# Two-layer attention kernel: attention weights times values by row halves, and a new order at the seams

## The chip, the core and the metric

The kernel runs on one core of a Trainium2 chip. A core has a matrix engine (TensorE, PE in the profile, with its weight loads as PEld), a vector engine (VectorE, DVE), a scalar engine (ScalarE, ACT), GpSimd (POOL) and SyncE (SP), which only starts transfers. Each engine works through its own list of instructions in order; engines wait for one another by semaphores. Transfers are started from the queues of SP, ACT and POOL and run on 16 DMA engines. Matmuls read SBUF and write PSUM, which has eight banks of 2 KB per partition; ACT and DVE read the results there.

The metric is the time of one execution on the device in microseconds (us). The clock granted to TensorE is given in the profile as a share of full speed.

## The reference

Two layers, each added to its input after a group normalisation, on two images of 256 channels and 64 x 64 positions, in float32. The first is full attention with 8 heads of 32 channels over all 4096 positions. The second has three parts, cut to what matters:

```
q, k, v = 1x1 convolutions of the normalised input (conv1, conv2, conv3)
fq, fk  = q, k plus a position term

# "lr": attention among the 64 blocks of 8 x 8 positions, for each place in a block
att   = softmax(fq^T fk / 16);  ctx = att v            # 64 groups of 64 tokens
feats = relu(bn(lr_W ctx))

# "sr": attention among the 64 positions of each block
qx = relu(bn(fq2 relu(bn(fq1 feats)))),  kx likewise,  vx = fv feats
ctx2   = softmax(qx^T kx / 16) vx                      # 64 groups of 64 tokens
feats2 = relu(bn(sr_W ctx2))

out = x + rate1 * feats2 + rate2 * depthwise_conv3x3(fc-mix of q, k, v)
```

## The kernel before

`direct_layers` does all of it; `general_layers` (the last third of the file) is compiled but only runs when a row sum of the first softmax falls out of range, which it doesn't here. For each image b the kernel goes through four stages: normalise and project (`group_stats`, `normalise`, `project0`), full attention (`attention0`), `layer1_first` with the lr attention, `layer1_second` with the sr attention and the convolution. The positions are cut into NT = 8 tiles of T = 512, the channels into KC = 2 chunks of P = 128.

Inside `manual_schedule` blocks the order of the PE instructions is the order of the code; elsewhere, and for the other engines, a scheduler places instructions by its own estimate of when their inputs are there. `issue_after(x)` holds what stands in it back until the instruction x. Where two blocks meet, the scheduler may set the first matmuls of the next among the last of the one before.

**group_attention** (line 982 on) handles eight groups of 64 tokens at once. It is a generator whose caller advances it, so that other work can be put between its steps. `sp` (L1012, with a small extra product of 5 rows, L1018) computes the scores, two groups at a time in the two column halves of the array. DVE and ACT make the softmax (L1028 to L1035). PE turns the weights (`at`, L1040), so that the tokens summed over lie on the partitions: two groups on partitions 0 to 63 and 64 to 127. DVE copies them in two instructions of 64 partitions (L1049) into `bd`, a block diagonal matrix for each pair w of groups: group 0's weights in the upper left, group 1's in the lower right, zeros elsewhere (set once by POOL). `pc` (L1058) is then, for each output chunk m and each pair w, one 128 x 128 by 128 product with `vs`, the values of both groups, in a bank for each m. Then `out(m, pc)` runs: ACT scales, shifts and clips (`bn_relu`, L1069) from PSUM into `feats` (lr) or `res` (sr). A float32 matmul is two pairs of instructions in the trace, so the 8 products of a group are 16 records. There are 8 calls per stage and image: 32 in all.

In the lr loop the call of tile t is interleaved with the projection `py` of tile t+2 (`project`, L1108) and with the `pc` of tile t-1. In the sr loop a tile first runs the q branch (`phq`, `prq`), perhaps a step of the convolution, the k branch (`phk`, `prk`), the attention, and more steps of the convolution at the places in `spots`. A convolution step is `mm` (L931), 16 products whose inputs `v` POOL prepares from the padded image `xp`, and whose results `z` DVE adds to the tiles of x (L936 to L958). Its weights `wf` are made by DVE, kept in DRAM and fetched at the first step of image 0 (sr tile 2); `pw` (L890) then mixes them on PE. `give(n)` (L1251) adds a finished tile of sr and starts the 512 KB output transfer.

**Seams.** `load_x` starts eight 512 KB loads on SP's queue. At the start POOL's queue carries the constants, 16 small loads of projection biases (L115) and then the first weights wqk. `fold_scores` (L186) multiplies weights w1, w2 and the position rows into one matrix for the lr scores; it stands after `project0` of image 0 and before its attention, and its first short part (`pt_place`, `pt_meet`, `pt_key`) is a chain between PE and ACT. `finish_last` ends the first attention: DVE takes the reciprocal of 128 x 512 row sums (L625) from ACT's copy `kept`, multiplies, adds x, and takes the last of the statistics; then `pm_l` and `pv_l` on PE turn statistics into mean and variance, and `firsts` are the first halves (chunk 0) of the first `py` products, put there for the time that normalising chunk 1 takes. `following` (L1349) starts the loads of image 1 in the last sr tile of image 0 and takes their statistics (`bn_stats`, L308, 16 instructions on DVE; aggregate L312).

Of the kernel before, what the change touches and what calls it, by code (L numbers as in the profile page):

```python
# [9 lines left out]
F32 = mybir.dt.float32  # L10
# [30 lines left out]
def direct_layers(ctx: ExitStack, tc: tile.TileContext, a: dict, out: bass.AP, bad: bass.AP):  # L41
# [34 lines left out]

    x_first = load_x(0)


    by_out = {}  # L80
    for name in ("w1", "w2"):
        by_out[name] = wpool.tile([P, KC, C], F32, tag="wp", name=f"{name}_by_out")

        for i in range(4):
# [4 lines left out]
            )  # L89
    place_rows = w4([4, C], "place_rows")  # L90
    nc.sync.dma_start(out=place_rows, in_=a["posq"])
    grid = const.tile([2, 64], F32, name="grid")
    nc.sync.dma_start(out=grid, in_=a["loc"][1:3, 0:64])
    meet = const.tile([2, P], F32, name="meet")
# [16 lines left out]
    for nm, col in (("wk0", V_BK0), ("wq0", V_BQ0)):  # L111
        b0[nm] = const.tile([P, 2], F32, name="b_" + nm)
        for h in range(NH0):
            r = HD0 * (h % 4)
            nc.gpsimd.dma_start(  # L115
                out=b0[nm][r : r + HD0, h // 4 : h // 4 + 1],
                in_=a["vecs"][64 * (h % 2) : 64 * (h % 2) + HD0, col + h // 2 : col + h // 2 + 1],
            )
# [67 lines left out]
    def fold_scores():  # L186


        wts["g"] = wpool.tile([P, KC, C], F32, tag="wp", name="wt_g_0")

# [24 lines left out]
        nc.tensor.matmul(pk, meet, grid, start=True, stop=True)  # L215
        nc.scalar.copy(at_key, pk)
        for k in range(KC):
            block = slice(k * P, (k + 1) * P)
            pg = bank([P, C + AT], f"pt_g_{k}")
            product(pg[:, 0:C], lambda j: by_out["w1"][:, j, block], lambda j: by_out["w2"][:, j, :])  # L220
            product(pg[:, C : C + 2], lambda j: by_out["w1"][:, j, block], lambda j: place[:, j, 1:3])
            product(pg[:, C + 2 : C + AT], lambda j: by_out["w2"][:, j, block], lambda j: part[:, j, :])
            nc.scalar.copy(wts["g"][:, k, :], pg[:, 0:C])
            nc.scalar.copy(w_at[:, k, 0:AT], pg[:, C : C + AT])
        nc.sync.dma_start(out=kept_w["g"], in_=wts["g"])

    outer = {}
# [59 lines left out]

    bd = const.tile([P, 4, 2, 64], F32, name="bd0")
    nc.gpsimd.memset(bd, 0.0)
    bds = [bd, bd]  # L290
    turn = [0]


    class Stats:
# [35 lines left out]

    def group_stats(xts, tagn):
        st = Stats(xts, tagn)
        for t in range(NT):
            for k in range(KC):
                st.tile(k, t)
        both, pv = slice(0, KC), bank([P, KC], f"pv_{tagn}")
        st.aggregate(both)
        st.means(both, bank([P, KC], f"pm_{tagn}"), nc.vector.tensor_copy)
        st.spread(both)
        st.variances(both, pv)  # L340
        st.deviations(both, pv)
        return st.mean, st.rstd

# [113 lines left out]
    def attention0(b, xts, held):  # L457
# [117 lines left out]
        def sum_rows(g, rows):  # L575
            if g == last:
                for j in SUMMED_LAST:
                    quarters(rows, ones, lambda u: unit(g, j, u), j == SUMMED_LAST[0], False)
                quarters(rows, ones, lambda u: acc[u], False, False)
            quarters(rows, ones, lambda u: added[g][u // 2][:, u % 2, :], g < last, True)  # L580

# [29 lines left out]
        def finish_last(g):  # L611
# [9 lines left out]
            st.shift = shift  # L621
            shift_of(st, 0)
            kept = w4([P, T], f"kept_{b}")
            nc.scalar.copy(kept, rows)
            nc.vector.reciprocal(avs[:, 1, :], kept)  # L625
            y = avs[:, 0, :]
            nc.scalar.copy(y, sums[g])
            nc.vector.tensor_mul(y, y, avs[:, 1, :])
            nc.vector.scalar_tensor_tensor(y, y, bv_last, held["x_last"], ALU.add, ALU.add)
# [351 lines left out]

    def group_attention(nm, q, k, tokens, wv, out, busy=False, apart=False, more=None):

# [60 lines left out]

        bd = bds[turn[0] % 2]
        turn[0] += 1
        for tt in range(2):
            rows = slice(64 * tt, 64 * tt + 64)
            nc.vector.tensor_copy(  # L1049
                bd[rows, :, tt, :].rearrange("p (a u) i -> p u a i", a=2), at[rows]  # L1050
            )
        if apart:
            values(1)
        yield
        for m in range(KC):
            pc = bank([P, T], f"pc_{nm}_{m}")
            for w in range(4):
                nc.tensor.matmul(  # L1058
                    pc[:, w * P : (w + 1) * P], vs[:, w, m * P : (m + 1) * P],
                    bd[:, w].rearrange("p a i -> p (a i)"), start=True, stop=True,  # L1060
                )
            out(m, pc)

# [4 lines left out]
    def bn_relu(dst, src, col, m):  # L1068
        nc.scalar.activation(  # L1069
            dst, src, AF.Relu, bias=vecs[:, col + 2 + m : col + 3 + m], scale=vecs[:, col + m : col + m + 1]  # L1070
        )


    def layer1_first(b, xts, put, check, st):
# [64 lines left out]
        with tc.manual_schedule(engines={E.PE, E.Activation, E.DVE}):  # L1139
# [14 lines left out]
            st.spread(second)  # L1154
            firsts = [lambda t=t, m=m: project(t, m, slice(0, 1)) for t in range(2) for m in range(KC)]
            if b:
# [20 lines left out]
        with tc.manual_schedule(engines={E.PE}):  # L1177

            before = None
            for t in range(NT + 1):  # L1180
                parts = None
                if t < NT:
                    def to_feats(m, pc, t=t):
                        bn_relu(
                            feats[m][:, :, t, :].rearrange("p o e -> p e o"),
                            pc.rearrange("p (e o) -> p e o", e=8), V_LR, m,
                        )

                    rows = slice(HD0 * (t % 4), HD0 * (t % 4) + AT)
                    parts = group_attention(  # L1190
                        f"lr_{b}_{t}", tiles.pop(t), source(t),
                        lambda c, w, t=t: source(t)[:, c, w * P : (w + 1) * P], wts["w3"], to_feats, b == 0,
                        more=(queries[rows, t // 4, :], keys[t // 4][rows, :], t == 0, t >= NT - 2),
                    )
                    next(parts)
                    if t == 3:
                        at_grid(1)
                for m in range(KC):
                    if t + 2 < NT:
                        project(t + 2, m, slice(0, KC))  # L1200
                    if before:
                        next(before, None)
                    if m == 0 and NT - 2 <= t < NT:
                        next(parts)
# [6 lines left out]
    def layer1_second(b, xts, feats, mean, rstd, shift, pacc, following):  # L1211
# [40 lines left out]
        def give(n):  # L1252
            res = results.pop(n)
            for m in range(KC):
                nc.vector.scalar_tensor_tensor(
                    res[:, m, :], res[:, m, :], wts["rate1"], xts[n][:, m, :], ALU.mult, ALU.add
                )
            nc.sync.dma_start(out=out[b, :, n * T : (n + 1) * T].rearrange("(k p) n -> p k n", p=P), in_=res)

        if b:  # L1260
            for t in range(3):
                to_image(t, True)
            ahead[0] = conv_transform(b, xp, *turns[0])
        pending = None
        for t in range(NT):
# [25 lines left out]
            with tc.manual_schedule(engines={mybir.EngineType.PE}):  # L1291
# [5 lines left out]
                for tt in images.get(t, ()):  # L1297
                    to_image(tt)
                if 0 in spots.get(t, ()):
                    conv()  # L1300
                if b == 0 and t == NT - 1:
                    for n in sorted(results):
                        give(n)
                k = branch("fk1", "fk2", V_FK1, V_FK2, "k")
                res = w4([P, KC, T], f"res_{nt}")

                def to_res(m, pc, res=res):

                    bn_relu(
                        res[:, m, :].rearrange("p (d o e) -> p o d e", d=8, o=8),  # L1310
                        pc.rearrange("p (o d e) -> p o d e", o=8, d=8), V_SRW, m,
                    )

                parts = group_attention(
                    nt, q, k, lambda c, w, f=f: f[c][:, w * P : (w + 1) * P], wts["fv"], to_res, apart=t + 1 < NT
                )
# [5 lines left out]
                else:  # L1322
                    next(parts)
                    if b == 0 and t == NT - 1:
                        following()
                    next(parts, None)
                if 2 in spots.get(t, ()):
                    conv()
# [20 lines left out]
    def following():  # L1349
        xts = load_x(1)  # L1350
        ahead.update(xts=xts, w0=load_layer0(1), stats=group_stats(xts, "l0_1"))

    for b in range(B):
        xts = x_first if b == 0 else ahead["xts"]
        w0 = w0_first if b == 0 else ahead["w0"]
        with tc.tile_pool(name=f"ps0_{b}", bufs=8, space=PSUM) as psum["ps"]:
            mean, rstd = group_stats(xts, "l0_0") if b == 0 else ahead["stats"]
            xn = apool.tile([P, KC, N], F32, tag="A", name=f"xn_{b}")
            for t in range(NT):
                for k in range(KC):  # L1360
                    normalise(xn[:, k, t * T : (t + 1) * T], xts[t][:, k, :], k, mean, rstd)
            held = project0(b, xn, w0)
            if b == 0:
                fold_scores()
        if b == 0:
# [569 lines left out]
```

## Time and profile before

| what | value |
|---|---|
| median of 3 runs | 3122.33 us (3120.56 to 3123.84) |
| profiled execution: its own time | 3121.84 us |
| its span, first to last instruction | 3120.1 us |
| mean granted clock of TensorE | 0.992 |
| attention of image 0, 110 to 1150 us: PE busy | 1035.70 of 1040.00 us |
| lr of image 0, 1150 to 1280: PE busy | 121.77 of 130.00 us |
| sr of image 0 with what follows, 1280 to 1660: PE busy | 365.40 of 380.00 us |
| attention of image 1, 1690 to 2705: PE busy | 1009.47 of 1015.00 us |

The profile is one execution, recorded by the chip. The span is cut into stages by time, and for each stage the table of windows gives the busy microseconds of each engine. A group line gives instructions of one line and shape with their number, and a second column with the shortest, median and longest duration in ns or the busy sum and mean. A wait line gives who waited for whom, and the total, number and longest of these waits. In a line in order of time the first number is the start, the second the length until the last record's end; the bracket is the idle time ahead of it, with what ended it.

### The profile page before, as it was taken

What the parts mean: (1) busy time and instruction counts of PE and PEld (TensorE: products, weight loads), DVE (VectorE), ACT (ScalarE), POOL (GpSimd) and SP (SyncE); (2) the same over time, 40 slices, a digit from 0 to 9 for tenths busy, and PEclk for the clock granted to TensorE, in tenths of its full rate; (3) what the DMA queues carried; (4) which work ended last, traced back from release to release, by engine and by line L of the source; (5) the groups of instructions that cost most, each with busy time, mean ns of one, the idle gap of its engine ahead of it and who ended that gap; (6) DMA issues with size and microseconds to landing.
All of it is one profiled execution on the core that took longest, in us unless ns stands there. A gap on an engine that the chain in (4) does not pass through costs nothing. (4 is left out here: it accounts for less than half of the span.)

```text
span 3120.1 us, 62504 instructions
## 1 busy us (share of the span) xinstructions
PE 3034.8 (97%) x25049; PEld 1830.3 (59%) x25049; DVE 2459.9 (79%) x3124; ACT 2314.6 (74%) x2437; POOL 844.6 (27%) x939
## 2 busy tenths in 40 slices
PE   7999999999999999999999999999999999899998
PEld 4555555555555556676764555555555555476765
DVE  4599988999989999846546998989999999834543
ACT  2699999999999983622237999999999999834333
POOL 3022222222222230155401222222222222305440
PEclk9999999999999999999999999999999999999999
DMA  7969679797897661230159687796888975700000
GB/s 257 262 127 181 143 154 173 150 177 155 168 181 159 127 139 32 77 132 27 41 200 262 127 173 153 155 178 137 177 165 162 182 151 126 166 4 4 21 14 22
DMA packets 243513, 424.39 MB, mean 136 GB/s; under 512 B 98840, under 2 KB 109644, under 8 KB 241036
## 3 DMA queue, kind: packets, MB, share of 16 engines
q0 software_dynamic: 95504, 238.36, 39.7%
q1 hardware_dynamic: 147708, 181.94, 21.6%
q8 instruction: 198, 3.24, 0.4%
q14 instruction: 103, 0.84, 0.1%
HBM read 119.03 MB, written 68.39 MB: 60 GB/s over the span
## 5 line engine op out<-in xcount | busy, mean ns | idle before, releaser
L551 DVE TENSOR_TENSOR e<-e,es 128x1024 f32<-128x1024 f32 (+1 forms) x956 | 1039.5, 1142 | 83.2 <-ACT es L504 81.4
L514 PE MATMUL av<-es,v 128*32 128x256 f32 (+1 forms) x9644 | 747.7, 390 | 0.0
L551 DVE TENSOR_TENSOR e<-e,v 128x1024 f32<-128x1024 f32 (+1 forms) x640 | 675.4, 1108 | 52.3 <-ACT v L504 51.2
L504 ACT ACTIVATE es<-sa 128x1536 f32<-128x1536 f32 (+1 forms) x444 | 636.0, 1432 | 94.6 <-PE sa L498 56.1
L498 PE MATMUL sa<-q,k 128*128 128x512 f32 x1736 | 562.2, 431 | 8.4 <-ACT avs L588 3.5
L514 PE MATMUL av<-v 128*32 128x256 f32 (+1 forms) x6228 | 506.5, 389 | 0.0
L514 PEld LDWEIGHTS av<-es,v 128*32 128x32 f32 x9644 | 316.3, 109 | 300.8 <-issue 162.6
L498 PEld LDWEIGHTS sa<-q,k 128*128 128x128 f32 x1736 | 280.5, 188 | 291.6 <-issue 136.3
L498 PE MATMUL sc<-q,k 128*128 128x512 f32 x1180 | 372.2, 397 | 2.1 <-ACT es L504 0.7
L498 PE MATMUL sb<-q,k 128*128 128x512 f32 x1180 | 371.6, 396 | 2.1 <-ACT v L504 2.1
L514 PEld LDWEIGHTS av<-v 128*32 128x32 f32 x6228 | 216.5, 109 | 178.7 <-issue 81.3
L504 ACT ACTIVATE es<-sc 128x1024 f32<-128x1024 f32 x296 | 306.5, 1036 | 0.0
L504 ACT ACTIVATE v<-sc 128x1024 f32<-128x1024 f32 x294 | 304.4, 1035 | 1.0 <-PE sa L498 0.9
L504 ACT ACTIVATE es<-sb 128x1024 f32<-128x1024 f32 x296 | 302.0, 1020 | 1.3 <-DMA acc<-es 1.3
L504 ACT ACTIVATE v<-sb 128x1024 f32<-128x1024 f32 x294 | 300.0, 1020 | 2.8 <-DMA acc<-v 2.8
L498 PEld LDWEIGHTS sb<-q,k 128*128 128x128 f32 x1180 | 221.8, 188 | 56.3 <-ACT v L504 2.5
L498 PEld LDWEIGHTS sc<-q,k 128*128 128x128 f32 x1180 | 211.4, 188 | 72.0 <-ACT es L504 9.4
L504 ACT ACTIVATE v<-sa 128x1536 f32<-128x1536 f32 (+1 forms) x146 | 209.3, 1434 | 35.6 <-PE sa L498 16.5
L931 PE MATMUL mm<-v,wf 128*128 128x256 f32 x1024 | 229.4, 382 | 5.1 <-DVE z L940 5.1
L561 POOL DMA_DIRECT2D es<-es x116 | 99.0, 854 | 478.7 <-ACT es L504 422.4
L931 PEld LDWEIGHTS mm<-v,wf 128*128 128x128 f32 x1024 | 194.4, 191 | 41.3 <-issue 12.0
L921 POOL TENSOR_TENSOR v<-col 128x512 f32<-128x512 f32 x128 | 164.9, 1314 | 194.5 <-DVE x L952 44.3
(262 smaller groups left out, 3173.9 us busy)
## 6 DMA issues: line engine op xcount, KB each, us to landing
acc<-es POOLq DMA_DIRECT2D x128, 512.0 KB, 6.4
acc<-v POOLq DMA_DIRECT2D x84, 512.0 KB, 6.3
es<-es POOLq DMA_DIRECT2D x136, 256.0 KB, 4.3
v<-es POOLq DMA_DIRECT2D x132, 256.0 KB, 5.0
k<-wk_halves SPq DMA_DIRECT2D x64, 512.0 KB
q<-wq_halves SPq DMA_DIRECT2D x256, 128.0 KB
v<-v POOLq DMA_DIRECT2D x90, 256.0 KB, 5.2
es<-v POOLq DMA_DIRECT2D x86, 256.0 KB, 4.1
```

Source lines behind the costliest of these rows:

```text
L498: nc.tensor.matmul(sc[:, i, :], held["k", g // 2][:, j * P : (j + 1) * P], held["q", g, u // 2][:, u % 2, :], start=True, stop=True,)
L504: nc.scalar.activation(dst, sc[:, i : i + m, :], AF.Exp, scale=SC0)
L514: nc.tensor.matmul(dst[HD0 * u : HD0 * u + HD0, n], lhs, rhs(u)[:, n], start=start, stop=stop)
L551: nc.vector.tensor_add(dst[:, s, :], dst[:, s, :], src)
L561: nc.gpsimd.dma_start(out=dst, in_=src, accum_op=ALU.add)
L921: (nc.gpsimd.tensor_add if plus else nc.gpsimd.tensor_sub)(dst, rows(one), rows(two))
L931: nc.tensor.matmul(mm[:, m, r, :], wf[:, k, 4 * r + q, m * P : (m + 1) * P], v[r // 2][:, r % 2, k, :], start=k == 0, stop=k == KC - 1,)
```

## The change

- `pc` by row halves. `bd` and its memset are gone. DVE copies `at` in one instruction into `turned`, 128 partitions by 256. The matmuls work on 64 rows of the array each: for each m and w, the group on partitions 0 to 63 and the one on 64 to 127, one after the other, 64 x 128 weights by 64 columns. The two halves write to different banks, and each bank holds both m. A group has 16 products instead of 8, and ACT's eviction of each m comes in two instructions of 128 x 256.
- `finish_last`: both reciprocals are of 128 x 256 and read PSUM; the row sums of the last group are made half by half; for image 1 the product reads PSUM without ACT's copy.
- The loads of `place_rows` and `grid` go ahead of those of w1 and w2 on SP; the 16 small bias loads of the start go from POOL's queue to ACT's.
- `fold_scores` is split: its first part stands before `project0`, the rest where it was.
- `firsts` holds three tiles instead of two.
- At sr tile 2 of image 0 the first convolution step stands after the k branch instead of before.
- `following` is split in steps; its statistics stand behind the last `give` before it (`issue_after`), its `pm_l` between the two m of the last `pc`. For image 1 the first three `to_image` stand behind the last eviction of lr.
- The last output tile goes out in two transfers, one for each m, from SP and ACT.

```diff
@@ group_attention
-        bd = bds[turn[0] % 2]
-        turn[0] += 1
-        for tt in range(2):
-            rows = slice(64 * tt, 64 * tt + 64)
-            nc.vector.tensor_copy(
-                bd[rows, :, tt, :].rearrange("p (a u) i -> p u a i", a=2), at[rows]
-            )
+        turned = small.tile([P, 2, 2, 64], F32, tag="turned", name=f"turned_{nm}")
+        nc.vector.tensor_copy(turned, at)
         if apart:
             values(1)
         yield
+        pc = [bank([P, KC, 4, 64], f"pc_{nm}_{tt}") for tt in range(2)]
         for m in range(KC):
-            pc = bank([P, T], f"pc_{nm}_{m}")
             for w in range(4):
-                nc.tensor.matmul(
-                    pc[:, w * P : (w + 1) * P], vs[:, w, m * P : (m + 1) * P],
-                    bd[:, w].rearrange("p a i -> p (a i)"), start=True, stop=True,
-                )
-            out(m, pc)
+                for tt in range(2):
+                    rows = slice(64 * tt, 64 * tt + 64)
+                    nc.tensor.matmul(
+                        pc[tt][:, m, w, :], vs[rows, w, m * P : (m + 1) * P], turned[rows, w % 2, w // 2, :],
+                        start=True, stop=True,
+                    )
+            for tt in range(2):
+                out(m, tt, pc[tt][:, m])
+            if m == 0 and between:
+                between()
@@ finish_last
+            for part in range(2):
+                n = slice(part * T // 2, (part + 1) * T // 2)
+                nc.vector.reciprocal(avs[:, 1, n], rows[:, n])
             kept = w4([P, T], f"kept_{b}")
-            nc.scalar.copy(kept, rows)
-            nc.vector.reciprocal(avs[:, 1, :], kept)
             y = avs[:, 0, :]
-            nc.scalar.copy(y, sums[g])
-            nc.vector.tensor_mul(y, y, avs[:, 1, :])
+            if b == 0:
+                nc.scalar.copy(y, sums[g])
+                nc.scalar.copy(kept, rows)
+                nc.vector.tensor_mul(y, y, avs[:, 1, :])
+            else:
+                nc.scalar.copy(kept, rows)
+                nc.vector.tensor_mul(y, sums[g], avs[:, 1, :])
@@ the 16 bias loads of the start
-            nc.gpsimd.dma_start(
+            nc.scalar.dma_start(
@@ layer1_first
-            firsts = [lambda t=t, m=m: project(t, m, slice(0, 1)) for t in range(2) for m in range(KC)]
+            firsts = [lambda t=t, m=m: project(t, m, slice(0, 1)) for t in range(3) for m in range(KC)]
...
-                        project(t + 2, m, slice(0, KC))
+                        project(t + 2, m, slice(1 if t == 0 else 0, KC))
@@ layer1_second
+            final = b == B - 1 and n == NT - 1
             for m in range(KC):
-                nc.vector.scalar_tensor_tensor(
+                kept["given"] = nc.vector.scalar_tensor_tensor(
                     res[:, m, :], res[:, m, :], wts["rate1"], xts[n][:, m, :], ALU.mult, ALU.add
                 )
-            nc.sync.dma_start(out=out[b, :, n * T : (n + 1) * T].rearrange("(k p) n -> p k n", p=P), in_=res)
+                if final:
+                    (nc.scalar if m else nc.sync).dma_start(out=halves[:, m, :], in_=res[:, m, :])
+            if not final:
+                nc.sync.dma_start(out=halves, in_=res)
...
-                if 0 in spots.get(t, ()):
+                if 0 in spots.get(t, ()) and (b or t > 2):
                     conv()
...
                 k = branch("fk1", "fk2", V_FK1, V_FK2, "k")
+                if b == 0 and t == 2:
+                    conv()
@@ following
-        xts = load_x(1)
-        ahead.update(xts=xts, w0=load_layer0(1), stats=group_stats(xts, "l0_1"))
+        ahead.update(xts=load_x(1), w0=load_layer0(1))
+        with tc.issue_after(kept["given"].ins):
+            steps = group_stats(ahead["xts"], "l0_1")
+            next(steps)
+        yield
+        next(steps)
+        yield
+        ahead["stats"] = next(steps)
+        yield
@@ main loop
+            fold = fold_scores() if b == 0 else iter(())
+            next(fold, None)
             held = project0(b, xn, w0)
-            if b == 0:
-                fold_scores()
+            next(fold, None)
```

## The prediction

> **What bounds the kernel now.** I read the busy share first, then the same shares cut into stages, then the waits of PE, and last the single groups around the changed matmuls.
>
> The first part of the page and the table by stage (window; length; busy microseconds of PE, PEld, DVE, ACT, POOL with counts; granted clock; DMA share; GB/s):
>
> ```profile
> PE 3034.8 (97%) x25049; PEld 1830.3 (59%) x25049; DVE 2459.9 (79%) x3124; ACT 2314.6 (74%) x2437; POOL 844.6 (27%) x939
> ...
> 2705.00:2830.00 125.00, 113.09 (x849) 75.50 (x840) 48.20 (x103) 57.38 (x74) 20.08 (x19) 0.96 0.12 43
> 2830.00:3121.00 291.00, 275.15 (x1289) 191.52 (x1287) 128.43 (x267) 93.97 (x166) 107.71 (x75) 0.98 0.04 16
> ```
>
> PE is the bound, also in the two stages that run `group_attention` (lr, 2705 to 2830, and sr, 2830 to 3121; the other image has them at 1150 and 1280), where no other engine is busy half the time. A microsecond in which PE stands there is a microsecond of the run. Where PE stood before:
>
> ```profile
> PE pw L890 <- DMA wf<-wf_kept: 5.1, 2, 4.6
> PE mm L931 <- DVE z L940: 5.1, 3, 3.8
> ...
> PE p_wk L400 <- DMA wqk<-in_wk_dram: 3.3, 1, 3.3
> ...
> PE pt_meet L206 <- ACT query_part L202: 1.8, 1, 1.8
> ```
>
> These (total, times, longest) are single waits at seams, some 49 us in all: all that reordering can win. The changed matmuls, from the groups of L1058 and from the order of time:
>
> ```profile
> L1058 PE MATMUL pc_lr<-bd,vs_lr x256: 272/275/422, 1201.8 to 2821.0; 128*128 128x128 f32 x128
> L1058 PE MATMUL pc_sr<-bd,vs_sr x256: 272/275/377, 1302.3 to 3108.6; 128*128 128x128 f32 x128
> ```
> ```profile
> 2762.72 1.95 PE L1058 MATMUL pc_lr<-bd,vs_lr 128*128 128x128 f32 x16
> 2764.60 0.45 PE L1012 MATMUL sp_lr<-xg,y 128*64 128x64 f32 x8
> 2764.98 0.33 PE L1018 MATMUL sp_lr<-keys,at 5*64 5x64 f32 x4
> ```
> ```profile
> 2763.82 2.25 ACT L1069 ACTIVATE feats<-pc_lr,vecs 128x512 f32<-128x512 f32 x2 [0.29 <-PE pc_lr L1058]
> ```
> ```profile
> L1069 ACT ACTIVATE feats<-pc_lr,vecs x32: 1177/1226/1273, 1202.9 to 2822.9; 128x512 f32<-128x512 f32 x32
> ...
> L1069 ACT ACTIVATE res_sr<-pc_sr,vecs x32: 777/778/780, 1303.9 to 3109.0; 128x512 f32<-128x512 f32 x32
> ```
>
> A group's 16 records take 1.88 us up to the next line's start. ACT empties m=0 while PE is already at m=1, in another bank; nothing waits.
>
> **The matmuls themselves.** 16 records of 128*128 weights by 128 columns become 32 of 64*128 weights by 64 columns, alternating between the row halves. Spacing by rows: 1.88/16 = 0.117 us for 128 columns of weights and 128 moved; L260 (128*128 weights, one moved column) runs its 8 records in 1.03 - 0.25 = 0.78 over 7 spacings, 0.111 us, so loading 128 weight columns alone sets that pace. L1012 (64 weight columns, 64 moved, two column halves) takes 1.15 us for 32. No row half is in the trace. Bounds for 32 records: 0.93 us if 64 moved columns set the pace (32 at L1012's rate), 16 x 0.111 = 1.78 if both halves load at once, 3.57 if loads follow one another. I take 1.78, nearest to L260, where weight columns decide: no gain. The ends are -27 and +57 us over 32 groups.
>
> [...]
>
> **A new wait.** A bank now holds one row half for both m. In the compiled order of the changed kernel, in all 32 groups, the first two matmuls of m=1 wait for ACT's evictions of m=0 from these banks. Queued behind them are the rest of m=1 and then the next group's scores. Price per lr group: end of the last m=0 matmul 0.25 us after its start, 0.10 to ACT's start (3.245 to 3.344 past 2900), two half evictions, 0.05 back, 0.10 for the first pair, less the usual 0.11. Half an eviction: the 8-column ACTIVATE of L965 takes 0.30 and follows another at 0.21; halving what lies above these, lr (1.226 long, 1.04 apart) gives 0.62 + 0.76 = 1.38 for two, sr (0.778) 0.45 + 0.54 = 0.99. So lr 1.77, sr 1.38. In 12 of 16 sr groups the order puts two `phq` records of 0.43 (0.86 us of the next group's work) into that hole: 0.52 remains. Sum 16 x 1.77 + 12 x 0.52 + 4 x 1.38 = **+40 us**. From below: L1031's 128x256 in 0.416 as a half's price gives +26; from above, evictions as long as now, +62.
>
> **Switches of tile shape.** Around L1012 in sr: 0.31 to its first start where the records before are 0.22 apart, and about 0.2 lost at the return: 0.35 a round trip. lr, where one side was a switch before, 0.2; sr 0.35, and 0.7 in the 12 groups with `phq` in between: 16 x 0.2 + 4 x 0.35 + 12 x 0.7 = **+13** (0 to +20).
>
> **Clock.** A wait of 2.08 us at 1703 was followed by half clock:
>
> ```profile
> 1664.70:1668.20 3.50, 2.57 (x10) 1.69 (x10) 0.00 (x0) 3.49 (x3) 0.00 (x0) 1.00 1.03 377
> ...
> 1705.30:1709.00 3.70, 3.70 (x24) 1.79 (x28) 1.50 (x2) 3.70 (x4) 1.12 (x3) 0.54 0.99 184
> ```
>
> while 1.57 at 1663 was not. 1.77 lies between; half clock for 3.4 us costs 1.7. I take three of 16 lr groups, **+5** (0 to +27).
>
> **One copy for two on DVE.** Two L1049 copies (0.42 each) become one of 128x256, by the 0.42 of DVE's L1030 on that size. PE waited for them at two lr ends and one sr end only: -0.4 each; the lr ends give -0.8. POOL's memset of bd was under other work: 0.
>
> **Seams.**
> - Conv in image 0, t=2: `pw` waited 4.57 us for wf. The k branch (16 records x 0.43 = 6.9 us) now goes ahead of it: -4.6, and the half clock of 1330.3 to 1333.3 goes (-1.7): **-6.3**. If wf came later by more than 2.3 us, part returns.
> - bn_stats of the next image: one stood on DVE at 1461.5 to 1466.0 waiting for its load, z behind it, PE 3.8 us behind z, then a clock of 0.61. All 16 now follow the last `give` but one: **-5.5**. The price comes after: 16 x 0.60 = 9.6 us and 3.0 of softmax after 1567.1 put the aggregate at 1580, not 1575.1; pm, which stands between m=0 and m=1 of the last group, is late, then m=1, its evictions and the sqrt table load (1.28) behind them on ACT, then p_wk: **+5** (+2 to +7).
> - Fold: from the last p_wq (106.7) to `sa` 9.15 us, 1.80 of it waiting and the end at half clock. What remains, 24 matmuls, some 3.3 at full clock and 0.53 for ACT: **-5.5** (-4 to -7). Its first part now stands ahead of the first p_wk and costs about 2.5 us there.
> - Start: 16 small loads go from POOL's queue to ACT's, so wqk (waited for until 21.9) lands earlier. But loads of x_0 now share their landing counters with these: x_0_2 to x_0_7 wait for earlier landings, where all eight were issued by 5.1 us without a wait. x_0_7 then lands some 2.3 us after its 14.86, DVE's stats and the first p_wk behind it, after the fold's first part: **+1.5** (-1 to +4). place_rows and grid on SP are 1 KB each: 0.
> - Reciprocal by halves from PSUM: DVE's 3.35 us (L625) starts earlier. Image 0: the product still waits for ACT's copy of avs, and pt_w now for kept (0.59) behind it: +0.3. Image 1: py waits for POOL's xg either way; the third pair of k=0 matmuls fills 1.25 us: **-1.4**.
> - The end: turned -0.4, last half output 256 KB for 512, at 374 GB/s -0.7: **-1.1**; its wait is counted above.
>
> **Sum.** 40 + 13 + 5 = +58; gains 6.3 + 5.5 + 5.5 + 1.4 + 1.1 + 0.8 = -20.6; +5 + 1.5 + 0.3 = +6.8. Together +44 on the profiled execution's own 3121.84 (span 3120.1; the runs' median, 3122.33, is 0.5 above): **3166 us**.
>
> **Rivals.**
> - B, halves at the pace of 64 moved columns: 27 less, 3139. For it: L1012's rate. Against: L260.
> - C, loads one after another: 57 more, 3223. For it: one PEld queue. Against: L1012's two column halves do overlap.
> - D, the other side, *streaming halves with short evictions*: body -27, no switch or clock cost, waits at their lower bound 26; with -20.6 + 6.8 that is -15: 3107. It decides once the groups' own sum (wait, switch, body) is under +14, 0.43 us a group. Against it: evictions would have to cost 0.42 against 0.54 and 0.76, besides the row halves.
> - The change does less than said: the 64-row records run as 128-row ones do, which is C's case.
>
> **Chances.** My forecast 0.62, B 0.12, C 0.11, D 0.12, nothing to be seen 0.03. This kernel's measurement tells 0.2% (6 us): faster 0.13, same 0.05, slower 0.82. Own range of the forecast 3145 to 3190; with B, half of D and the upper bounds of wait and clock, 3115 to 3205; C is left out.
>
> **What would show it.** Between m=0 and m=1 of `pc_lr` about 1.8 us without PE, released by ACT's feats, in sr about 0.5 to 1.4; 32 records of `pc` in about 1.8 us of issue; `pw` and `mm` gone from the long waits; p_wk of image 1 later after its softmax. I am wrong if PE's waits for feats and res sum to under 20 us, or if `pc` takes 0.9 or 3.6 us a group.

## The result, and the profile after

| | median us | runs | ratio to before (95%) | span of the profile | granted clock |
|---|---|---|---|---|---|
| before | 3122.36 | 3120.56 to 3123.84 | | 3120.1 | 0.992 |
| changed | 3194.19 | 3191.74 to 3197.84 | 1.0228 (1.0216 to 1.024) | 3191.6 | 0.976 |

The change costs 72 us. The prediction was 3166 with a range of 3115 to 3205: slower, as forecast, but by 72 us where the sum gave 44. The measured time lies above the forecast's own range (3145 to 3190), and inside the wider one only because that took in the upper bounds of wait and clock.

The first part of the page of the changed kernel (busy time of the engines, and the clock in 40 slices):

```profile
PE 3097.9 (97%) x25641; PEld 1869.3 (59%) x25641; DVE 2444.3 (77%) x3094; ACT 2327.3 (73%) x2500; POOL 836.7 (26%) x922
...
PEclk9999999999999998889999999999999999979999
```

PE is busy 63 us longer than before, with 592 records more. Its clock is below 0.9 in slices 16 to 18 and 36 of 40 (79.8 us each), where it was above in every slice before. They lie in lr of image 0 and the beginning of its sr, and in lr of image 1. The lr stage of image 1, from its `pm_l` to the first `phq`, in the changed kernel and then in the kernel before (window; length; busy PE, PEld, DVE, ACT, POOL; clock; DMA share; GB/s):

```profile
2757.00:2895.00 138.00, 125.93 (x885) 87.67 (x885) 34.25 (x79) 50.07 (x79) 6.08 (x12) 0.81 0.07 28
```
```profile
2718.70:2824.00 105.30, 100.33 (x756) 70.80 (x756) 37.52 (x87) 43.91 (x59) 6.68 (x13) 0.98 0.07 28
```

The stage is 33 us longer, PE stands 12 us in it instead of 5, and the clock is 0.81 where it was 0.98. What PE waited for (total, times, longest):

```profile
PE pm_l L312 <- DVE mv_l L309: 32.7, 3, 25.9
PE pc_lr L1068 <- ACT feats L1082: 14.5, 16, 1.3
PE at_sr L1052 <- DVE e_sr L1047: 3.6, 2, 2.5
...
PE p_wk L401 <- ACT rstd_l L325: 3.1, 1, 3.1
```

The waits of `pw` for wf and of `mm` for z have left the head of the list. New are `pc_lr` behind ACT's feats in all 16 groups, `at_sr` behind a softmax, and a first `pm_l` that starts at 25.9 us instead of 16.7.

To see where the 71.5 us between the two spans went, I cut both traces at the first record of each stage (lr of image 0 begins at its first `py`, lr of image 1 at its `pm_l`):

| stretch, us | before | changed | difference |
|---|---|---|---|
| start, up to the first `p_wk` | 22.0 | 30.3 | +8.3 |
| projection and fold of image 0 | 93.9 | 88.7 | -5.2 |
| attention of image 0, up to the first `py` | 1054.4 | 1055.9 | +1.5 |
| lr, image 0 | 105.7 | 132.6 | +26.9 |
| sr, image 0 | 304.3 | 317.1 | +12.8 |
| projection and attention, image 1 | 1138.4 | 1132.6 | -5.8 |
| lr, image 1 | 105.4 | 137.8 | +32.4 |
| sr, image 1 | 295.9 | 296.7 | +0.8 |

59 of the 71.5 us are in the two lr stages. One group of lr in the changed kernel, PE's rows in order of time (start, duration, and in brackets the visible wait with its releaser):

```profile
2791.24 1.11 PE L1068 MATMUL pc_lr<-turned_lr,vs_lr 64*128 64x64 f32 x16
2793.21 1.65 PE L1068 MATMUL pc_lr<-turned_lr,vs_lr 64*128 64x64 f32 x16 [0.86 <-ACT feats L1082]
2794.79 0.45 PE L1024 MATMUL sp_lr<-xg,y 128*64 128x64 f32 x8
...
2798.39 5.72 PE L1006 MATMUL pvs_lr<-wt_w,xg 128*128 128x256 f32 x16
2803.94 1.88 PE L1121 MATMUL py<-xg,wt_g 128*128 128x512 f32 x4
```

The group takes 3.55 us up to the next line's start, where it took 1.88. Where nothing waits (e_late below), the same 32 records take 1.93, and the second 16 start 0.94 after the first. Here the second 16 start 1.03 later than that and take another 0.59 longer, because the pair's second half waits for its own bank: 1.62 us of hole. ACT's row shows the two evictions that PE waits for; the second ends at 2793.71, and the matmul that waits for it starts at 2793.76:

```profile
2792.38 1.33 ACT L1082 ACTIVATE feats<-pc_lr,vecs 128x256 f32<-128x256 f32 x2 [0.44 <-PE pc_lr L1068]
```

And then `pvs_lr`, which nothing in the change touches, takes 5.72 us. In the kernel before it took:

```profile
2767.17 3.72 PE L994 MATMUL pvs_lr<-wt_w,xg 128*128 128x256 f32 x16
```

The table of windows over this one period of 16.45 us of the changed kernel says why (columns as above):

```profile
2792.28:2795.64 3.36, 2.38 (x36) 1.97 (x36) 0.00 (x0) 2.27 (x4) 0.00 (x0) 1.00 0.00 0
2795.64:2802.47 6.83, 6.83 (x46) 5.32 (x43) 1.87 (x5) 1.07 (x3) 0.00 (x0) 0.50 0.00 0
2802.47:2808.73 6.26, 6.26 (x34) 3.77 (x32) 1.12 (x2) 1.51 (x3) 0.00 (x0) 1.00 0.00 0
```

Behind the hole come 6.83 us at half clock, in which PE is busy without a break. The clock record of the trace has such stretches of 6.83 us from 2795.64, 2812.71, 2829.77, 2846.84 and 2863.91, behind five groups in a row. Over both lr stages half clock rose from 13.2 to 96.4 us.

### The profile page after: what moved, and what is told of

It is laid out like the page before. It is cut to its first block, busy times and chain, and to the rows that moved or that the text cites. A ratio compares the mean times of both kernels' runs of the same rounds, so it can differ in the third digit from the quotient of the medians.

```text
span 3191.6 us, 63707 instructions
## 1 busy us (share of the span) xinstructions
PE 3097.9 (97%) x25641; PEld 1869.3 (59%) x25641; DVE 2444.3 (77%) x3094; ACT 2327.3 (73%) x2500; POOL 836.7 (26%) x922
## 3 DMA queue, kind: packets, MB, share of 16 engines
q1 hardware_dynamic: 147580, 181.68, 21.1%
```

## The experiments

Medians and ratios are against runs of the kernel before on the same chip (3120.99, 3121.9, 3120.56 and 3122.01 us in the four sets).

| run | us | ratio to before (95%) |
|---|---|---|
| e_late: both evictions after both blocks | 3128.14 | 1.0019 (1.0009 to 1.0029) |
| e_quad: and 64 x 64 tiles | 3108.44 | 0.995 (0.9933 to 0.9967) |
| e_diag: block-diagonal `pc` as before, all seams new | 3116.84 | 0.999 (0.998 to 1.0) |
| e_start: changed kernel, small loads back on POOL | 3190.4 | 1.0212 (1.0193 to 1.0231) |
| e_fill: changed kernel, dummy products in the hole | 3159.65 | 1.0116 (1.0098 to 1.0134) |
| e_best: e_quad, small loads back on POOL | 3099.32 | 0.9927 (0.9912 to 0.9941) |
| e_conv: e_best, convolution at t=2 where it was | 3098.23 | 0.9922 (0.9908 to 0.9936) |
| e_only: kernel before with 64 x 64 tiles alone | 3100.8 | 0.993 (0.9916 to 0.9943) |
| e_fold: e_only and the fold in two parts | 3106.86 | 0.9959 (0.9946 to 0.9973) |
| e_seam: block diagonal, seams new but the start's small loads and the convolution | 3110.48 | 0.9968 (0.9957 to 0.9978) |
| e_fold2: e_fold and the two early loads | 3097.1 | 0.9919 (0.9905 to 0.9932) |

**e_late: is it the wait, or the row halves?** From the changed kernel:

```diff
@@ group_attention
-            for tt in range(2):
-                out(m, tt, pc[tt][:, m])
             if m == 0 and between:
                 between()
+        for m in range(KC):
+            for tt in range(2):
+                out(m, tt, pc[tt][:, m])
```

> The changed kernel, with the four evictions of a group moved behind the matmuls of both m: no matmul of m=1 waits for an eviction of m=0; row halves and everything else stay. Theory (the idle time between the two m costs twice: 0.9 to 1.7 us a group, and the half clock that follows it in lr, 44 and 58 us of half clock in the two lr stages): PE's waits for feats nearly vanish, the clock in lr is full again, a group of pc takes 1.8 to 2.1 us, and the time is 3120 to 3135. Rival (work on half the rows counts as little work, and that lowers the clock): the waits vanish but the half clock in lr stays, and only some 20 us come back: 3165 to 3180.

66 us of the 72 go. The group runs through, and `pvs_lr` is back at its old length. PE's rows of this run:

```profile
2786.57 2.00 PE L1068 MATMUL pc_lr<-turned_lr,vs_lr 64*128 64x64 f32 x32
2788.50 0.45 PE L1024 MATMUL sp_lr<-xg,y 128*64 128x64 f32 x8
...
2791.07 3.72 PE L1006 MATMUL pvs_lr<-wt_w,xg 128*128 128x256 f32 x16
```

32 records take 1.93 us up to the next line's start (2788.50 - 2786.57), against 1.88 for the 16 block-diagonal ones. The row halves themselves neither gain nor cause half clock: the two lr stages have 20.2 us of it, the changed kernel 96.4.

**e_quad: a shape that does gain.** From e_late:

```diff
-                    nc.tensor.matmul(
-                        pc[tt][:, m, w, :], vs[rows, w, m * P : (m + 1) * P], turned[rows, w % 2, w // 2, :],
-                        start=True, stop=True,
-                    )
+                    for cc in range(2):
+                        cols = slice(m * P + 64 * cc, m * P + 64 * cc + 64)
+                        nc.tensor.matmul(
+                            pc[tt][64 * cc : 64 * cc + 64, m, w, :], vs[rows, w, cols],
+                            turned[rows, w % 2, w // 2, :], start=True, stop=True,
+                        )
```

> As e_late, and each product of 64 rows is also cut into two column halves of 64 weights (four tiles of 64x64, 32 products for a group, 64 records). Theory (loading the 128 weight columns sets the pace of the row halves, 0.111 us for a pair of them): with 64 columns to load the pace is that of the scores, 0.058 us for a set of tiles, and a group of pc takes about 0.93 us instead of 1.78: 27 us less than e_late. Rival (records are issued at no more than one in about 0.03 us, or something else sets the pace): a group takes 1.8 us or more, time as e_late or above.

The same work as 64 records in four quarters of the array (PE's rows of this run):

```profile
2780.89 1.16 PE L1070 MATMUL pc_lr<-turned_lr,vs_lr 64*64 64x64 f32 x64
2781.98 0.45 PE L1024 MATMUL sp_lr<-xg,y 128*64 128x64 f32 x8
```

1.09 us a group instead of 1.93, where 0.93 was expected. This fits the prediction's reading of L260 (0.111 us a record with 128 columns) and L1012 (1.15 us for 32 records with 64), that the columns of the weights set the pace; no run halves them in any other way. The time falls by 20 us; 32 groups times 0.84 would be 27, and where the rest went is open. This beats the kernel before.

**e_diag: the seams without the row halves.**

```diff
@@ from the changed kernel: pc, bd and its two copies, to_feats and to_res as in the kernel before
-        turned = small.tile([P, 2, 2, 64], F32, tag="turned", name=f"turned_{nm}")
-        nc.vector.tensor_copy(turned, at)
+        for tt in range(2):
+            rows = slice(64 * tt, 64 * tt + 64)
+            nc.vector.tensor_copy(bd[rows, :, tt, :].rearrange("p (a u) i -> p u a i", a=2), at[rows])
...
```

> The changed kernel with the products of weights and values as they were before (block diagonal, 128 rows, a bank for each m, one eviction for each m); all other parts of the change stay. Theory (the lr stages, 59 of the 71 us, lost by the new products alone, and the seams together win a little: start +8.3, fold -5, the rest below nothing): 3108 to 3120, no half clock within lr. Rival (the new order at the seams brought the half clock of lr): it stays above 3150.

All seams together win 4 us (0 to 6 by the interval), so everything the changed kernel lost, and about 4 us more, comes from `pc` with its evictions and its copy.

**e_fill: does the idle time itself pull the clock down?** The evictions stay between the blocks. PE gets work that nobody reads:

```diff
@@ group_attention, changed kernel
             for tt in range(2):
                 out(m, tt, pc[tt][:, m])
+            if m == 0 and nm.startswith("lr"):
+                fill = bank([P, T], f"fill_{nm}")
+                for i in range(7):
+                    nc.tensor.matmul(
+                        fill[:, 0:P], vs[:, i % 4, 0:P], vs[:, i % 4, P : 2 * P], start=True, stop=True,
+                    )
```

> The changed kernel with seven dummy products (128x128 by 128 columns, float32, into a bank that nothing reads) between the two column blocks of the weighted values in the first attention stage of layer 1 (lr), so that PE works where it waited for the feats evictions. Seven at about 0.235 us (8 of the same shape took 1.88 us in the kernel before) are 1.65 us, about the 1.7 us of the waits: the evictions still set when the second block starts, so the waits' own 16 x 1.7 = 27 us stay. Theory (the idle time makes the granted clock fall to half, and the half clock costs the rest of what lr lost): half clock in the two lr stages falls from 96 us to under 25, and the kernel takes 3160 to 3175 us. Rival (the half clock comes from the tile shapes or from the total work, or the loss in lr is the waits alone): half clock in lr stays above 70 us and the time stays at 3187 to 3200 us.

Held, at the lower edge: 3159.65. One period of this run, PE's rows, then the clock of the period from the table of windows:

```profile
2774.73 1.11 PE L1068 MATMUL pc_lr<-turned_lr,vs_lr 64*128 64x64 f32 x16
2775.77 1.83 PE L1077 MATMUL fill_lr<-vs_lr 128*128 128x128 f32 x14
2777.53 1.11 PE L1068 MATMUL pc_lr<-turned_lr,vs_lr 64*128 64x64 f32 x16
...
2781.14 3.72 PE L1006 MATMUL pvs_lr<-wt_w,xg 128*128 128x256 f32 x16
```
```profile
2774.70:2788.40 13.70, 13.70 (x121) 10.26 (x120) 2.99 (x7) 4.88 (x8) 0.00 (x0) 1.00 0.00 1
```

The second block starts 1.76 us after the end of the first, later than in the changed kernel, and still the period is 13.70 us and not 16.45. PE does more and is done sooner. Half clock in the two lr stages falls to 13.8 us, and they take 241.4 us together where the changed kernel takes 270.4. So 29.0 us of lr's loss was the clock, and it was the standing still that called it: here the evictions stay and the hole is filled, in e_late the hole is gone without a filler, and both times the half clock goes. A group with the filler is 0.3 us longer than with the hole, 4.6 us over 16 groups, so the clock's share is rather 33.6. Two other ways lie near: the 59.3 us that lr lost against the kernel before, less 16 times the 1.67 us by which a group of `pc` became longer, are 32.6; the 54.9 us that it lost against e_late, less 16 times 1.62, are 28.9. Some 29 to 34 us, then.

**e_start and e_best: the start.** One line, in the changed kernel and in e_quad:

```diff
-            nc.scalar.dma_start(
+            nc.gpsimd.dma_start(
                 out=b0[nm][r : r + HD0, h // 4 : h // 4 + 1],
```

> The changed kernel with the 16 small bias loads of the start back on POOL's queue. Theory (x_0_4 to x_0_7 were issued at 8.9 to 14.6 us instead of by 4.6 because their landing counters are shared with the small loads on ACT's queue, and the first p_wk starts at 30.3 instead of 22.0 for that): all x loads are issued by 5 us, the statistics are ready near 17 us, the first p_wk starts at 23 to 25 us, and 5 to 7 us come back: 3187 to 3190. Rival (the statistics are late for contention among the transfers): no more than 2 us.

> The quadrant version (four 64x64 tiles, evictions after both blocks; 3108.4 us) with the 16 small bias loads back on POOL's queue. Theory (the first p_wk came 8 us late because x's loads share landing counters with the small loads on ACT's queue): first p_wk at 22 us instead of 30, and 3100 to 3105 us, since in the changed kernel the same edit won 8.1 us at the start and 3.8 us in all. Rival (the start is given back wholly in the attention that follows): 3107 to 3110 us.

In both, the first `p_wk` is back at 22 us. SP's queue shows the cause: the eight loads of x, first in the changed kernel, then in e_best (start, time until the last of the eight is issued):

```profile
0.73 14.33 SPq L70 DMA_DIRECT2D x<-in_x_dram  x8
```
```profile
0.74 4.19 SPq L70 DMA_DIRECT2D x<-in_x_dram  x8
```

In the changed kernel the last load of x is issued only near 15 us, since x's loads and the small loads on ACT's queue share landing counters (the semaphores that tell that a transfer has landed). The traces give their numbers at each issue. In the kernel before the eight loads of x have one each (101, 110 to 113, 115 to 117), and none waits. In the changed kernel the 16 small loads have 100, 111 to 113, 115 and 116, and x's loads 102 and 114 (three each), 115 and 116. Six of the eight loads of x carry a wait for the counter of an earlier transfer there, four for a load of x (102, 114) and two for a small one (115, 116). The waits of SP's queue in the first 30 us of the changed kernel (total, times, longest):

```profile
SPq L70 <- DMA x<-in_x_dram: 10.8, 4, 4.3
```

In e_best some 7 to 9 us of the 9 at the head show in the whole time (3108.44 to 3099.32, but on another chip; the ratios, 0.995 to 0.9927, give 7, and their intervals overlap). In e_start only 3.8 of 8.1 do, and later stretches take nearly 6 us more than in the changed kernel's trace; the two intervals overlap, so this difference is not settled.

**e_conv: the convolution step at t=2.** From e_best:

```diff
-                if 0 in spots.get(t, ()) and (b or t > 2):
+                if 0 in spots.get(t, ()):
                     conv()
...
-                if b == 0 and t == 2:
-                    conv()
```

> The kernel of the run before this one in the list (quadrants, small loads on POOL) with the convolution of step t=2 of the first image back where the kernel before had it, ahead of the second key branch. My prediction's step: the new place is worth 6.3 us, so this is 6 us slower than that run. Theory now: the new place gained the 4.6 us wait of pw for wf, and gave it back as a wait of the transposes for e_sr (2.5 us) and the half clock that followed it, since VectorE's adds of the convolution were stretched to about 1 us each beside POOL's adds just ahead of the softmax; then this run is within 3 us of that one, its 2.5 us wait of at_sr is gone and the wait of pw is back.

1.1 us apart, inside the scatter: the new place is worth nothing that these runs can tell. The changed kernel shows what it brought with it (POOL, DVE and PE, order of time):

```profile
1387.80 5.08 POOL L932 TENSOR_TENSOR v<-col 128x512 f32<-128x512 f32 x4 [11.98 <-PE sp_sr L1024]
1388.33 7.45 DVE L963 SCALAR_TENSOR_TENSOR x<-z,edges,x 128x128 f32<-128x128 f32 x7
1395.70 0.41 DVE L1040 TENSOR_REDUCE nm_sr<-sp_sr 128x4 f32<-128x256 f32 x1
...
1398.20 0.44 PE L1052 MATMUL at_sr<-ident,e_sr 128*128 128x128 f32 x2 [2.50 <-DVE e_sr L1047]
```

Seven adds of the convolution take 7.45 us, the first five of them beside POOL's work; in e_conv seven of them, at 1337.45 when POOL stands still, take 1.92. The softmax is queued behind them on DVE, and PE stands 2.5 us. With the old place that wait is down to 1.1. What I expected wrongly is that the wait of `pw` for the load of wf returns: it is in the waits neither of e_conv nor of e_only, which has the old order everywhere (`pw` waits 0.3 us there, for DVE).

**e_only, e_seam: do the parts add?** e_only is the kernel before with `turned`, the 64 x 64 tiles and late evictions of e_quad, and nothing else. e_seam is e_diag with the two edits of e_best and e_conv.

> The kernel before with nothing but the weighted values by quadrants (four 64x64 tiles, one copy of the transposed weights instead of two, evictions after both blocks, by halves): none of the new orders at the seams. Theory (the parts add): the seams as a whole were worth 4 us in the block-diagonal version (3116.8 against 3121.0), and quadrants were worth 8.4 us against that version, so this takes 3111 to 3115 us. Rival (products saved of 32 groups x 0.79 us all count): 3096 us. Rival (quadrants win only together with the new seams): 3118 to 3123 us.

> The opposite: block-diagonal weights as in the kernel before, all new orders at the seams but two, which are as in the kernel before (the small bias loads on POOL's queue, the convolution of step t=2 ahead of the second key branch). Theory (the seams' gains are real and overlap in part with those of the quadrants, which already removed the 4.6 us wait for wf and let the second image's attention begin earlier): 3106 to 3112 us, 9 to 15 below the kernel before, of which 8 are the late start of the block-diagonal run with all seams (3116.8) taken back. Rival (the seams are worth the 2 to 3 us that they add to the quadrants): 3117 to 3120 us.

64 x 64 tiles alone win 21.1 us, nearer to the 25 of all saved products than to my sum; the seams alone win 10.1. Together (e_conv) they win 23.7, not 31. A part of the overlap can be named: the wait for wf, 4.6 us before and 2.5 in e_seam, is gone in e_only, with the tiles alone; how they remove it was not followed up. The rest is open.

**e_fold, e_fold2: the one seam that stays.** From e_only; e_fold has the first and last part of this, e_fold2 all:

```diff
@@ fold_scores: two steps
         nc.scalar.copy(at_key, pk)
+        yield
...
@@ e_fold2 only: the loads of place_rows and grid (4 lines) right behind x_first = load_x(0)
...
@@ main loop
+            fold = fold_scores() if b == 0 else iter(())
+            next(fold, None)
             held = project0(b, xn, w0)
-            if b == 0:
-                fold_scores()
+            next(fold, None)
```

> The kernel before with the weighted values by quadrants (3100.8 us) and one of the seams: fold_scores in two parts, its first before the projection of the first image, its second after. Theory (this is the one seam that pays: in the traces its second part took 4.1 us in place of 6.1, and the stretch that holds its first part lost 2.4): 3095 to 3098 us. Rival (the seams' gains are inside the scatter of runs): 3100 to 3102 us.

> The run with quadrants and the fold in two parts (3106.9 us), and with it the loads that its first part reads, place_rows and grid, right behind the loads of x, as in the changed kernel. Theory (in that run the fold's first part waited 11.9 us for place_rows, which SP issued only at 21.41 us, behind the eight loads of w_by_out; the fold's new order itself is worth some 4 to 5 us): first p_wk at 21 to 23 us, and 3094 to 3098 us, below quadrants alone (3100.8) and at or below the best so far (3098.2). Rival (the new order of the fold brings nothing in the end): 3100 to 3102 us.

Alone, the fold's new order loses 6 us. PE's first row of it in e_fold, and SP's queue:

```profile
30.61 0.34 PE L194 MATMUL pt_place<-ident,place_rows 4*128 4x4 f32 x2 [11.94 <-POOL masks L179]
```
```profile
21.41 0.52 SPq L91 DMA_DIRECT2D place_rows<-in_posq_dram  x1
```

The wait is put down to POOL's masks, but in e_fold2 `pt_place` runs at 18.50, before POOL writes any of these masks (25.61 and later). What it waits for is its own input, place_rows, issued only at 21.41 behind eight loads of w_by_out. With that load moved ahead the first `p_wk` is at 21.0 and the run takes 3097.1, 3.7 below e_only, which ran on another chip; the intervals of the two ratios overlap, so this gain is not settled. It is the lowest time found, with e_conv (3098.23) beside it; their intervals overlap too.

## Why the prediction was right in kind and short in size

| step of the prediction | it said | the runs show | from |
|---|---|---|---|
| body of `pc`, 64-row halves | 0 (1.78 us a group) | 1.93 for 1.88 before | e_late |
| wait for the evictions, lr | 28.3 | 16 x 1.62 = 25.9 | a group of the changed kernel less one of e_late |
| wait for the evictions, sr | 11.8 | 8.3, some half clock in it | the two sr stretches, changed less e_late |
| switches of tile shape, body included | 13 | 11.3, with all else in which the two differ | e_late less e_diag |
| clock | 5 (0 to 27) | 29 to 34 in lr | e_fill |
| start | 1.5 (-1 to 4) | 8.3 | first `p_wk` |
| the other seams, -20.6 + 5 + 0.3 | -15.3 | -12.5 | e_diag (-4.2) less the start's 8.3 |

The measured column, with 31 for the clock, sums to +72; the medians are 71.8 apart. Three rows are differences between runs, so this tests only the split of what e_late took away, 66 us, into waits and clock (65). The 1.2 us that the prediction gave to `turned` are in the last row's forecast and not in e_diag.

**The wait.** Right in place, cause and about in size. Half an eviction took 0.77 us in lr and 0.56 in sr (medians) where 0.76 and 0.54 were reckoned for the second of two. One of my own marks misled: I would be wrong, it said, if the waits for feats and res summed to under 20 us. The list has 14.5 + 1.9. It counts the 0.86 us ahead of each second block, but not the 0.59 inside it, where PE's rows are only drawn apart. The length of the group shows both.

**The clock.** This is the step that failed: "I take three of 16 lr groups, +5 (0 to +27)". It came from two single waits, 2.08 us followed by half clock and 1.57 not, as if a threshold lay between them, and from 3.4 us at half clock for a fall. Each piece of the changed kernel's hole, 1.03 and 0.59 us, is shorter than either wait, and yet the clock record has 14 falls behind the 16 lr groups, of 6.6 us on average, where the kernel before has one of 3.41. Even my upper bound, all 16 groups at 1.7 us, is too low. The half-clock stretches of lr in the changed kernel last 3.41, 6.83 or 10.24 us, whole multiples of 3.41. In the 3.36 us ahead of the fall at 2795.64 PE was busy for 2.38: less than a third of them idle was enough. The idle share alone does not decide. In the kernel before, PE was idle for 1.29 of the 3.42 us from 1660.98 on, a part of the wait of 1.57, and the clock stayed:

```profile
1660.98:1664.40 3.42, 2.13 (x5) 0.58 (x4) 1.49 (x3) 1.37 (x2) 0.00 (x0) 1.00 1.04 387
```

What else counts stays open.

**The start.** The mechanism stood in the prediction: shared landing counters make the loads of x wait (10.8 us in four waits). The size did not: I had x's last load land 2.3 us late, and SP issued it some 10 us late (at 14.58 us for 4.60). The first `p_wk` came 8.3 us later, outside the -1 to +4 of this term.

**The convolution's place.** I priced it by the wait it removes. That wait is gone, and in e_conv and e_only it is gone without the new place as well; and the step's own adds on DVE came to stand ahead of a softmax (2.5 us).

**The fold.** -5.5 was predicted, -3.7 found in e_fold2, which is not clear of the scatter. "1 KB each: 0" for the two early loads (4.0 and 0.5 KB by the trace of the changed kernel, 0.45 and 0.24 us to issue) was right for their cost and overlooked that the gain hangs on them: without them it is +6.

**The rivals.** B and D (a pace set by 64 columns) fell with 1.93 us a group, C (3.57) too. In the changed kernel alone C could not have been told apart: a group takes 3.55 us there, and only e_late shows that nearly half of it is the wait. Two row halves take 0.121 us a pair in e_late, one full tile took 0.117, and 128 columns of weights with one moved column 0.111 (L260): both halves at once, but each as slow as its columns. With four quarters the columns are halved too, and the group takes 1.09.

## What to carry to other kernels

When PSUM banks are cut another way, look for the eviction that now lies between two matmuls, and write every product of a bank before the first eviction of it; here that one reordering was worth 66 us. A hole in the matrix engine that comes back in every group can cost more than its length, as here (25.9 us of holes in lr, 29 to 34 of clock): price the clock after it as well, and test it with dummy work in the hole. Splitting the array paid here where it cut the columns of the weights (1.09 us a group for 1.88), not where it cut the rows alone (1.93), and a moved step needs its loads moved with it.

## What the runs showed of the hardware

- Holes of 1.03 and 0.59 us, once in some 16 us of the changed kernel's lr, were enough for half clock, in stretches of whole multiples of 3.41 us; filled with 1.76 us of dummy products (e_fill), the period shrank from 16.45 to 13.70 us.
- 64 float32 records of 64 x 64 weights by 64 columns over the four quarters take 1.09 us (e_quad); 32 of 64 x 128 take 1.93 (e_late), 16 of 128 x 128 by 128 take 1.88 (before).
- DVE's scalar_tensor_tensor `x<-z,edges,x` (128 x 128) took 0.34 to 0.35 us in all 103 cases of the changed kernel in which POOL ran no TENSOR_TENSOR beside it, and 0.75 to 1.42, at the median 1.35, in the ten that lay wholly beside one. The slowing was seen, not tested by itself.
